# Attention then two 3x3 convolutions: the large attention pools on the other side of memory, and the last block's end put between the first bands

## The chip, the cores and the metric

The kernel runs on one core of a Trainium2 chip. The metric is device time in microseconds (us) of one execution, the median of several runs. The engines are named as in the profile: PE (TensorE, matmuls), PEld (its weight loads), DVE (VectorE), ACT (ScalarE), POOL (GpSimd) and SP (SyncE, which here only issues transfers).

## The reference

The input x has 4 images of 128 channels and 64 x 64 pixels, in float32. Two layers follow one another.

```python
# layer 0: attention with 4 heads of 32 channels over 4096 positions, scale = 32 ** -0.5
x_norm = group_norm(x, 8 groups)
q, k, v = split(qkv_w @ x_norm + qkv_b)
attn = softmax(q @ k.T * scale)
x = x + proj_w @ (attn @ v) + proj_b
# layer 1: a residual block of two 3x3 convolutions with weights quantized to 3 bits
residual = x
out = relu(batchnorm(conv3x3(x, quant(w1, alpha1))))     # statistics over batch and pixels
out = batchnorm(conv3x3(out, quant(w2, alpha2)))
return relu(out + residual)
```

## The kernel before

**Attention** runs over 32 blocks: 4 images, and in each 8 blocks of 512 queries. A block has 32 steps of 128 keys. In a step PE computes the scores of four heads (L442), ACT takes their exponential into a tile p of 128 x 4 x 512 (L444), and PE multiplies p with the values into `acc` (L456). The denominators of the softmax are sums of the p tiles over the steps. DVE adds most of them into a tile r (L469, L471); the p tiles of six steps (`MOVED`) are added by transfers that POOL issues, into a tile rm (L464, L466). The program's order is written out by hand: three halves of scores, then three halves of weights, and side work hung on half steps by `schedule` with `at_half` and `add`. The end of each block is side work of the next: `merge` adds rm to r by a transfer, `sums` multiplies r with ones on PE in two halves, ACT copies the result to `ls`, `spread` brings 4 rows of 512 into 128 x 16 by a transfer (lq), `invert` takes reciprocals (rq) and writes them to DRAM (rd), `gather` reads them back on all partitions (rc), `weigh` multiplies acc's copy with rc, `project` is the output projection on PE, and `store` adds bias and input on DVE and writes to `y0` in DRAM through POOL. The last block has no next one. For it `sums_at_once` runs totals of rm and r on PE and reciprocals of 128 x 512 on DVE, and `bounds` takes two maxima for the check value `worst`.

**Convolution layer 1** works on 16 bands (4 images, 4 bands of 16 rows). A band's input is split into a high and a low part. A plain band (`conv`, L828) takes 36 matmuls of 512 columns: two half bands, 9 taps, two parts. A mixed band (`conv_by_two`, L874) computes two rows at once from sums and differences of rows and takes 24. `mixed_parts` makes its inputs: vo and vi on DVE (L595 to L598), their high parts uo and ui on ACT (L600), the low parts lo and li on DVE (L604). `rows_of_two` puts the result together: a copy on ACT (L884), inner rows (L887, L888) and outer rows (L891, L893) on DVE; the squares for the batch norm follow on ACT (L957). A plain band takes its statistics on DVE (L969) and is copied by ACT (L970). The set `BY_TWO` says which bands are mixed; in the first layer before, band 2 is plain. The loop in `layer` prepares band m + 2 in the pass of band m (`parts_of`) and loads band m + 3 (`load_band`, on SP with border memsets on POOL).

**The seam** stands at L837 to L855. Bands 0 and 1 are convolved between the parts of the last block's end, band 2 is split, and then `att.close()` gives all attention pools back at once. The pools `mid` (results cv0 to cv3, the second layer's weights, the mixed weights `wmix`, the statistics) and `upper` (parts of mixed bands) take their memory. `mix_weights(0)` and six small operations on alpha (L904 to L906) follow, and then the loop. The pass of band 5 contains `count_bad`, with one small matmul `nbad` on PE (L1004).

**Memory.** Pools are allocated as a stack. A pool can be put on the left or on the right side (`side="right"`), each a stack of its own. By default an instruction that uses a new pool waits until everything in the released pools that it overlays is done; `reuse_waits="tile"` makes it wait only for the tiles that it overlays. The tiles of `kpool` (keys in attention, bands afterwards) stay in place throughout.

Of the kernel before, what the change touches and what calls it, by code (L numbers as in the profile page):

```python
# [78 lines left out]
def _fast_body(ctx, tc, x, norm_w, norm_b, qkv_wt, qkv_b, proj_wt, proj_b,  # L79
# [131 lines left out]
    y0 = [dram.tile([P, N], F32, name=f"y0_{b}") for b in range(B)]  # L211
    BR = 2 * RB
    KW = (BR + 2) * PW
    att = ExitStack()
    vpool = att.enter_context(tc.tile_pool(name="vpool", bufs=NB + 1))
    qpool = att.enter_context(tc.tile_pool(name="qpool", bufs=2))
    stage = att.enter_context(tc.tile_pool(name="stage", bufs=1))
    xpool = att.enter_context(tc.tile_pool(name="xpool", bufs=3))
    ppool = att.enter_context(tc.tile_pool(name="ppool", bufs=9))
# [253 lines left out]
    def finish_parts(n):  # L473

        b, qb = blocks[n]
        av = rpool.tile([P, FB], F32, name=f"av{n}", tag="av")
        rc = rpool.tile([P, FB], F32, name=f"rc{n}", tag="rc")
        t = {}

        def copy():  # L480
            nc.scalar.copy(av, acc[n])


        def total(r, first, end, cs=slice(0, FB)):
            if "l" not in t:
                t["l"] = psa.tile([P, FB], F32, name=f"l{n}", tag="a")
            for h in range(HEADS):
                nc.tensor.matmul(t["l"][h * D : (h + 1) * D, cs], ones, r[:, h, cs],  # L488
                                 start=first, stop=end)

        def merge():
            nc.gpsimd.dma_start(out=rsum[n], in_=msum[n], accum_op=ALU.add)  # L492

        def evacuate():
            t["ls"] = stage.tile([P, FB], F32, name=f"ls{n}", tag="ls")
            nc.scalar.copy(t["ls"], t["l"])
# [7 lines left out]
        def sums_at_once():  # L504
            total(msum[n], True, False)
            total(rsum[n], False, True)
            evacuate()
            for j in range(4):
                cs = slice(j * P, (j + 1) * P)
                nc.vector.reciprocal(rc[:, cs], t["ls"][:, cs])  # L510
            weigh()

        def bounds():
            most = [small.tile([P, 1], F32, name=f"most{i}") for i in range(2)]
            for u, m in zip((t["ls"], rc), most):
                nc.vector.tensor_reduce(m, u, AX.X, ALU.max)
                nc.vector.tensor_tensor(worst[:, 0:1], worst[:, 0:1], m, ALU.add)
# [14 lines left out]

        def gather():
            nc.sync.dma_start(out=rc, in_=t["rd"].unsqueeze(1).to_broadcast([HEADS, D, FB]))

        def weigh():
            nc.vector.tensor_tensor(av, av, rc, ALU.mult)

        def residual():
            t["x"] = load_x(b, qb)  # L540

        def project():
            t["o"] = psa.tile([P, FB], F32, name=f"po{n}", tag="a")
            banded(t["o"], wp, av)

        def store():
            nc.vector.scalar_tensor_tensor(t["x"], t["o"], bp, t["x"], ALU.add, ALU.add)
            nc.gpsimd.dma_start(out=y0[b][:, qb * FB : (qb + 1) * FB], in_=t["x"])

        return dict(copy=copy, merge=merge, sums=sums, sums_at_once=sums_at_once, bounds=bounds,  # L550
                    spread=spread, invert=invert, gather=gather,
                    weigh=weigh, residual=residual, project=project, store=store)

# [26 lines left out]

    BY_TWO = (set((3, 4, 6, 7, 9, 10, 12, 13, 14)), set((2, 3, 4, 6, 7, 9, 10, 12, 13, 14)))

    def mixed_parts(t, name):

# [94 lines left out]
    def schedule(n, before):  # L681
# [49 lines left out]
        if b + 1 < B:  # L731
# [8 lines left out]
                    at_half(ends[13 + 2 * i], late[b][1 + 2 * i])  # L740
                    at_half(ends[13 + 2 * i] + 3, late[b][2 + 2 * i])
            if qn == 2:
                at_half(ends[1], late[b][5])
                at_half(ends[1] + 1, late[b][6])
                at_half(ends[1] + 1, late[b][7])
                at_half(ends[1] + 2, late[b][8])
            if b == 0:
                chunks = {2: (), 3: (0, 1), 4: (2, 3), 5: (4, 5), 6: (6,), 7: (7,)}
            else:
# [108 lines left out]
    def mix_weights(i):  # L858

# [35 lines left out]

        return copy, inner, outer

    mix_weights(0)


    a_q, a_g, a_n = ([small.tile([P, 1], F32, name=f"{n}{i}") for i in range(2)]
                     for n in ("aq", "ag_", "an"))
    for i in range(2):
# [16 lines left out]
        nc.vector.tensor_tensor(a, r, a_g[i], ALU.mult)  # L920
        return a, c

    def layer(i, prepare, done):


        plain = [m for m in range(len(bandlist) - 1) if m not in BY_TWO[i]]
# [6 lines left out]
        n_plain, n_two = (float(len(u) * 2 * FB) for u in (plain, two))  # L933
        nc.gpsimd.memset(end[:, 0:1], n_plain)
        nc.gpsimd.memset(end[:, 3:4], n_two)
        for m, (b, g) in enumerate(bandlist[:-1]):
            begin, rest, later = prepare(m)
            if m in BY_TWO[i]:
                a = conv_tile(i, b, g)
                a = [a[:, j, :] for j in range(2)]  # L940
                if (len(two) - 1 - two.index(m)) % 2:
                    c = [psa.tile([P, FB], F32, name=f"c{i}_{b}_{g}{j}", tag="a") for j in "xy"]
                else:
                    c = pss.tile([P, 2, FB], F32, name=f"c{i}_{b}_{g}z", tag="s")
                    c = [c[:, j, :] for j in range(2)]
                conv_by_two(ready[i, b, g], a, c, i)
# [13 lines left out]
            ps = done[m] if m < len(done) else conv_tile(i, b, g)  # L960
            for j in range(2):
                if m >= len(done):
                    conv(ready[i, b, g], ps[:, j, :], j, wq[i])
            begin()
            rest()
            later()
            for j in range(2):
                c = 2 * g + j
                nc.vector.bn_stats(st[:, 2 * plain.index(m) + j, :], ps[:, j, :])  # L969
                nc.scalar.copy(cv[b][:, c * FB : (c + 1) * FB], ps[:, j, :])  # L970
            if m == 0:
                mv = small.tile([P, 2], F32, name=f"first{i}", tag="mv")
                nc.vector.bn_aggr(mv, st[:, 0:2, :].rearrange("p j s -> p (j s)"))
                nc.vector.tensor_copy(shift[:, 0:1], mv[:, 0:1])
                nc.vector.tensor_scalar(shift[:, 1:2], mv[:, 0:1], -1.0, None, ALU.mult)
# [21 lines left out]
    def count_bad():  # L997
# [6 lines left out]
        nc.tensor.matmul(nbad[0:1, 0:1], bad, ones[:, 0:1], start=True, stop=True)  # L1004
        nc.vector.tensor_copy(cnt, nbad[0:1, 0:1])

    def nothing():
        pass

    def first(m):  # L1010
        begin = rest = nothing
        if 0 < m and m + 2 < len(bandlist):
            begin, rest = parts_of(0, m + 2, raw[bandlist[m + 2]])

        def later():
            if m == 5:
                count_bad()
                raw["w"] = f32(stack_tile("raw_w"))[:, : TAPS * P].rearrange("p (t o) -> p t o", o=P)
                nc.sync.dma_start(out=raw["w"], in_=wqd)
            if m == 6:  # L1020
                nc.vector.tensor_copy(wq[1], raw["w"])
            if 0 < m < len(bandlist) - 3:
                load_band(*bandlist[m + 3])

        return begin, rest, later

    a1, c1 = layer(0, first, early)

    def relu_band(m):
        b, g = bandlist[m]  # L1030
# [29 lines left out]

    def load_res(b, i):
        if b < B - 2:
            t = mid.tile([P, HN], F32, name=f"res{b}_{i}")
# [18 lines left out]

        return begin, rest, later

    a2, c2 = layer(1, second, [])
    for b in (B - 2, B - 1):
        for i in range(4):
            load_res(b, i)
# [469 lines left out]
```

## Time and profile before

| | |
|---|---|
| median of 3 runs | 2505.38 us (2503.05 to 2505.57) |
| profiled execution | 2506.32 us, of which the span in the trace is 2504.6 us |
| PE, DVE, ACT busy | 98%, 88%, 86% of the span |
| attention ends (first conv matmul) | 2234.4 us |
| first convolution layer's last matmul ends | 2359.9 us |
| mean granted PE clock | 0.994 |

The span runs from the first to the last instruction in the trace. Times in the trace are counted from its start. The profiled execution lies 0.9 us above the median of the runs, so differences are taken against its own time and then carried to the median.

### The profile page before, as it was taken

The page shows a single profiled execution, that of the slowest core. Times are in us where ns is not written, and L with a number is a line of the kernel's source. Part 1 is how long each engine was busy: PE and PEld are TensorE (multiplying, and loading weights), DVE is VectorE, ACT ScalarE, POOL GpSimd, SP SyncE. Part 2 cuts the span into 40 slices and gives each one's busy share as a digit, 9 for nine tenths or more (in the row PEclk, how much of TensorE's full clock was granted, in tenths as well). Part 3 has the DMA queues.
Part 4 walks back from the last instruction along what each step waited for, and adds up shares of the span by engine and source line. Part 5 has one row for each costly group of instructions (what it writes and reads, how often), then busy time and mean ns, then how long its engine had stood idle before and what let it go on. Part 6 is the DMA issues. An engine that isn't in the chain of part 4 may idle for free. (4 is left out here: it accounts for less than half of the span.)

```text
span 2504.6 us, 64822 instructions
## 1 busy us (share of the span) xinstructions
PE 2459.0 (98%) x28480; PEld 1462.1 (58%) x28480; DVE 2206.2 (88%) x1552; ACT 2147.0 (86%) x2344; POOL 281.9 (11%) x463
## 2 busy tenths in 40 slices
PE   9999999999999999999999999999999999998995
PEld 6555555555555555555555555555555555566774
DVE  6899888898988888889988898889999999988797
ACT  5999888999988899999988898998999999964475
POOL 2111111111011111110011111110000000100000
PEclk9999999999999999999999999999999999999998
DMA  6777677787767666788767767688656656664205
GB/s 197 189 185 170 163 178 174 171 200 184 181 156 168 178 165 165 160 201 191 167 149 184 167 157 170 170 204 185 147 129 153 142 131 148 154 128 97 86 1 203
DMA packets 148954, 403.84 MB, mean 161 GB/s; under 512 B 59416, under 2 KB 60184, under 8 KB 120120
## 3 DMA queue, kind: packets, MB, share of 16 engines
q0 software_dynamic: 45840, 280.39, 49.0%
q1 hardware_dynamic: 100952, 113.60, 17.2%
q8 instruction: 225, 3.69, 0.6%
q10 hardware_dynamic: 1872, 5.64, 0.6%
q14 instruction: 65, 0.53, 0.1%
HBM read 107.48 MB, written 56.42 MB: 65 GB/s over the span
## 5 line engine op out<-in xcount | busy, mean ns | idle before, releaser
L444 ACT ACTIVATE p<-s 128x1024 f32<-128x1024 f32 x2048 | 1950.5, 1032 | 202.2 <-PE s L442 154.0
L471 DVE TENSOR_TENSOR r<-r,p 128x2048 f32<-128x2048 f32 x768 | 1758.2, 2289 | 65.3 <-ACT p L444 15.0
L442 PE MATMUL s<-q,k 64*128 64x512 f32 x8192 | 1139.7, 409 | 1.9 <-ACT p L444 1.7
L456 PE MATMUL acc<-p,v 128*32 128x256 f32 x16384 | 1026.6, 383 | 0.0
L442 PEld LDWEIGHTS s<-q,k 64*128 64x128 f32 x8192 | 715.7, 185 | 410.9 <-issue 166.1
L456 PEld LDWEIGHTS acc<-p,v 128*32 128x32 f32 x16384 | 462.8, 109 | 483.4 <-issue 248.4
L466 POOL DMA_DIRECT2D rm<-p x160 | 139.1, 869 | 799.4 <-ACT p L444 556.8
L352 DVE SCALAR_TENSOR_TENSOR kst<-pk,b,kst 128x512 fp32r<-128x512 f32 x32 | 24.0, 750 | 83.3 <-PE s L442 68.5
L469 DVE TENSOR_TENSOR r<-p,p 128x2048 f32<-128x2048 f32 x32 | 73.2, 2288 | 12.8 <-ACT p L444 12.8
L352 DVE SCALAR_TENSOR_TENSOR qst<-pq,b,qst 128x512 fp32r<-128x512 f32 x32 | 24.0, 751 | 58.5 <-PE s L442 47.5
L957 ACT ACTIVATE uo<-cv,shift 128x1024 fp32r<-128x1024 f32 x19 | 21.9, 1153 | 53.1 <-DVE cv L893 50.5
L356 POOL DMA_DIRECT2D qd<-qst x31 | 23.6, 761 | 266.7 <-DVE qst L352 225.3
L828 PE MATMUL c<-hi,wq 128*128 128x512 f32 x198 | 51.2, 403 | 1.2 <-ACT hi L1045 1.2
L828 PE MATMUL c<-lo,wq 128*128 128x512 f32 x198 | 50.8, 401 | 0.0
L492 POOL DMA_DIRECT2D r<-rm x31 | 26.2, 844 | 218.2 <-PE s L442 61.8
L970 ACT COPY cv<-c 128x512 f32<-128x512 f32 x22 | 12.9, 586 | 38.4 <-DVE st L969 38.4
L828 PEld LDWEIGHTS c<-hi,wq 128*128 128x128 f32 x198 | 36.9, 188 | 13.1 <-issue 2.1
L828 PEld LDWEIGHTS c<-lo,wq 128*128 128x128 f32 x198 | 37.3, 188 | 10.0
L874 PE MATMUL c<-ui,wmix 128*128 128x512 f32 x114 | 35.2, 418 | 6.8 <-ACT cv L970 4.2
L356 POOL DMA_DIRECT2D kd<-kst x27 | 20.0, 740 | 178.6 <-DVE kst L352 169.9
L351 ACT ACTIVATE kst<-pk,b 128x512 fp32r<-128x512 f32 x32 | 22.3, 699 | 18.1 <-PE pk L317 18.0
L488 PE MATMUL l<-r,ones 128*32 128x256 f32 (+1 forms) x504 | 37.7, 383 | 0.0
(258 smaller groups left out, 1137.1 us busy)
## 6 DMA issues: line engine op xcount, KB each, us to landing
rm<-p POOLq DMA_DIRECT2D x192, 1024.0 KB, 7.8
q<-qd SPq DMA_DIRECT2D x248, 128.0 KB
r<-rm POOLq DMA_DIRECT2D x31, 1024.0 KB, 7.6
x<-in_x_dram SPq DMA_DIRECT2D x86, 256.0 KB
k<-kd SPq DMA_DIRECT2D x124, 128.0 KB
qd<-qst POOLq DMA_DIRECT2D x31, 512.0 KB, 5.6
kd<-kst POOLq DMA_DIRECT2D x27, 512.0 KB, 4.7
y<-x POOLq DMA_DIRECT2D x32, 256.0 KB, 6.1
```

Of the source, the lines that this page charges most:

```text
L352: nc.vector.scalar_tensor_tensor(lo, ps[what], bias, t[:, 0, :], ALU.add, ALU.subtract)
L356: (nc.sync if start else nc.gpsimd).dma_start(out=dst[b, j].rearrange("s p n -> p s n"), in_=t)
L442: nc.tensor.matmul(s[:, i, :], k[r, half, c0 : c0 + P], q[r, half, part, :], start=(part == 0), stop=(part == 1))
L444: nc.scalar.activation(pts[step][:, 2 * half : 2 * half + 2, :], s, AF.Exp, scale=SCALE)
L456: nc.tensor.matmul(acc[n][h * D : (h + 1) * D, cs], v[:, kt % KB, h * D : (h + 1) * D], pt[:, h, cs], start=(kt == 0 and half == 0), stop= ...
L466: nc.gpsimd.dma_start(out=msum[n], in_=pt, accum_op=ALU.add)
L469: nc.vector.tensor_tensor(rsum[n], pts[step - 1], pt, ALU.add)
L471: nc.vector.tensor_tensor(rsum[n], rsum[n], pt, ALU.add)
L488: nc.tensor.matmul(t["l"][h * D : (h + 1) * D, cs], ones, r[:, h, cs], start=first, stop=end)
L492: nc.gpsimd.dma_start(out=rsum[n], in_=msum[n], accum_op=ALU.add)
L828: nc.tensor.matmul(ps.rearrange("p (r w) -> p r w", w=W), w[:, tap, :], part[:, r0 + kh : r0 + kh + RB, kw : kw + W], start=(n == 0), stop ...
L874: nc.tensor.matmul(ps.rearrange("p (r w) -> p r w", w=W), w[:, kw, :], part[m][:, :, kw : kw + W], start=(n == 0), stop=(n == 5))
```

## The change

1. vpool, qpool and ppool (values, queries, p tiles) go to the right side, in a stack of their own (`core`), which is released first. `mid`, now with two results cv0 and cv1, and `upper` are allocated there with waits by tile. The results cv2 and cv3 and the residual tiles go to a pool `low` on the left, allocated after the rest of attention has been given back, in the pass of band 3.
2. The last block's end uses the same steps as the other blocks (merge, sums, spread, invert, gather, weigh), in a function `opening` that places them between the work on bands 0, 1 and 2. Project and store come in the pass of band 3.
3. Band 2 of the first layer is mixed.
4. Four small side tasks of the group norm (`late[b][5]` to `late[b][8]`) move by a few half steps.

```diff
-    att = ExitStack()
-    vpool = att.enter_context(tc.tile_pool(name="vpool", bufs=NB + 1))
-    qpool = att.enter_context(tc.tile_pool(name="qpool", bufs=2))
+    core, att = ExitStack(), ExitStack()
+    vpool = core.enter_context(tc.tile_pool(name="vpool", bufs=NB + 1, side="right"))
+    qpool = core.enter_context(tc.tile_pool(name="qpool", bufs=2, side="right"))
+    ppool = core.enter_context(tc.tile_pool(name="ppool", bufs=9, side="right"))
...
-    BY_TWO = (set((3, 4, 6, 7, 9, 10, 12, 13, 14)), set((2, 3, 4, 6, 7, 9, 10, 12, 13, 14)))
+    BY_TWO = (set((2, 3, 4, 6, 7, 9, 10, 12, 13, 14)), set((2, 3, 4, 6, 7, 9, 10, 12, 13, 14)))
...
-                at_half(ends[1], late[b][5])
-                at_half(ends[1] + 1, late[b][6])
-                at_half(ends[1] + 1, late[b][7])
-                at_half(ends[1] + 2, late[b][8])
+                at_half(ends[0], late[b][5])
+                at_half(ends[0] + 1, late[b][6])
+                at_half(ends[2], late[b][7])
+                at_half(ends[2] + 1, late[b][8])
...
-    early = [conv_tile(0, *bandlist[m]) for m in range(2)]
-    last = parts[len(blocks) - 1]
-    conv(ready[0, 0, 0], early[0][:, 0, :], 0, wq[0])
-    last["residual"]()
-    conv(ready[0, 0, 0], early[0][:, 1, :], 1, wq[0])
-    split_band(*bandlist[2])
-    load_band(*bandlist[3])
-    last["sums_at_once"]()
-    conv(ready[0, 0, 1], early[1][:, 0, :], 0, wq[0])
-    conv(ready[0, 0, 1], early[1][:, 1, :], 1, wq[0])
-    last["project"]()
-    last["store"]()
-    last["bounds"]()
-    att.close()
-    mid = ctx.enter_context(tc.tile_pool(name="mid", bufs=1))
-    cv = [mid.tile([P, N], F32, name=f"cv{b}") for b in range(B)]
+    core.close()
+    mid = ctx.enter_context(tc.tile_pool(name="mid", bufs=1, side="right", reuse_waits="tile"))
+    cv = [mid.tile([P, N], F32, name=f"cv{b}") for b in range(2)]
     wq.append(mid.tile([P, TAPS, P], F32R, name="wq1"))
-    upper = ctx.enter_context(tc.tile_pool(name="upper", bufs=12))
     wmix = mid.tile([P, 2, 3, P], F32R, name="wmix")
+    upper = ctx.enter_context(tc.tile_pool(name="upper", bufs=12, side="right", reuse_waits="tile"))
...
-    mix_weights(0)
...
+        def stats(m, j, ps):
+            nc.vector.bn_stats(st[:, 2 * plain.index(m) + j, :], ps[:, j, :])
+        def keep(m, j, ps):
+            nc.scalar.copy(cv[b][:, c * FB : (c + 1) * FB], ps[:, j, :])
...
         def later():
+            if m == 3:
+                last = parts[len(blocks) - 1]
+                last["project"]()
+                last["store"]()
+                att.close()
+                pools["low"] = ctx.enter_context(tc.tile_pool(name="low", bufs=1, reuse_waits="tile"))
+                cv.extend(pools["low"].tile([P, N], F32, name=f"cv{b}") for b in (2, 3))
...
+    def opening(banks, stats, keep, origin):
+        last = parts[len(blocks) - 1]
+        last["merge"]()
+        e = [conv_tile(0, *bandlist[m]) for m in range(2)]
+        conv(ready[0, 0, 0], e[0][:, 0, :], 0, wq[0])
+        begin, rest = parts_of(0, 2, raw[bandlist[2]])
+        begin()
+        load_band(*bandlist[3])
+        stats(0, 0, e[0])
+        keep(0, 0, e[0])
+        conv(ready[0, 0, 0], e[0][:, 1, :], 1, wq[0])
+        mix_weights(0)
+        rest()
+        last["residual"]()
+        stats(0, 1, e[0])
+        keep(0, 1, e[0])
+        origin()
+        conv(ready[0, 0, 1], e[1][:, 0, :], 0, wq[0])
+        last["sums"](0)
+        last["sums"](1)
+        last["spread"]()
+        begin, rest = parts_of(0, 3, raw[bandlist[3]])
+        begin()
+        load_band(*bandlist[4])
+        conv(ready[0, 0, 1], e[1][:, 1, :], 1, wq[0])
+        stats(1, 0, e[1])
+        keep(1, 0, e[1])
+        last["invert"]()
+        last["gather"]()
+        rest()
+        stats(1, 1, e[1])
+        keep(1, 1, e[1])
+        done = banks(2)
+        conv_by_two(ready[0, 0, 2], *done, 0)
+        begin, rest = parts_of(0, 4, raw[bandlist[4]])
+        begin()
+        last["weigh"]()
+        rest()
+        load_band(*bandlist[5])
+        return {0: None, 1: None, 2: done}
```

More of the change, by code (lines that the diff above doesn't have):

```diff
@@ L213, in _fast_body @@
     KW = (BR + 2) * PW
-    att = ExitStack()
-    vpool = att.enter_context(tc.tile_pool(name="vpool", bufs=NB + 1))
-    qpool = att.enter_context(tc.tile_pool(name="qpool", bufs=2))
+    core, att = ExitStack(), ExitStack()
+    vpool = core.enter_context(tc.tile_pool(name="vpool", bufs=NB + 1, side="right"))
+    qpool = core.enter_context(tc.tile_pool(name="qpool", bufs=2, side="right"))
+    ppool = core.enter_context(tc.tile_pool(name="ppool", bufs=9, side="right"))
     stage = att.enter_context(tc.tile_pool(name="stage", bufs=1))
     xpool = att.enter_context(tc.tile_pool(name="xpool", bufs=3))
-    ppool = att.enter_context(tc.tile_pool(name="ppool", bufs=9))
     rpool = att.enter_context(tc.tile_pool(name="rpool", bufs=1))
@@ L501, in sums @@
                 evacuate()
[L504 to L517, printed above, removed]
         def spread():
@@ L548, in store @@
             nc.gpsimd.dma_start(out=y0[b][:, qb * FB : (qb + 1) * FB], in_=t["x"])
-        return dict(copy=copy, merge=merge, sums=sums, sums_at_once=sums_at_once, bounds=bounds,
+        return dict(copy=copy, merge=merge, sums=sums,
                     spread=spread, invert=invert, gather=gather,
@@ L921, in batch_norm, with layer @@
         return a, c
-    def layer(i, prepare, done):
+    def layer(i, prepare, start=None):
         plain = [m for m in range(len(bandlist) - 1) if m not in BY_TWO[i]]
@@ L935, in layer, with origin, banks @@
         nc.gpsimd.memset(end[:, 3:4], n_two)
+        def stats(m, j, ps):
+            nc.vector.bn_stats(st[:, 2 * plain.index(m) + j, :], ps[:, j, :])
+        def keep(m, j, ps):
+            b, g = bandlist[m]
+            c = 2 * g + j
+            nc.scalar.copy(cv[b][:, c * FB : (c + 1) * FB], ps[:, j, :])
+        def origin():
+            mv = small.tile([P, 2], F32, name=f"first{i}", tag="mv")
+            nc.vector.bn_aggr(mv, st[:, 0:2, :].rearrange("p j s -> p (j s)"))
+            nc.vector.tensor_copy(shift[:, 0:1], mv[:, 0:1])
+            nc.vector.tensor_scalar(shift[:, 1:2], mv[:, 0:1], -1.0, None, ALU.mult)
+        def banks(m):
+            b, g = bandlist[m]
+            a = conv_tile(i, b, g)
+            if (len(two) - 1 - two.index(m)) % 2:
+                c = [psa.tile([P, FB], F32, name=f"c{i}_{b}_{g}{j}", tag="a") for j in "xy"]
+            else:
+                c = pss.tile([P, 2, FB], F32, name=f"c{i}_{b}_{g}z", tag="s")
+                c = [c[:, j, :] for j in range(2)]
+            return [a[:, j, :] for j in range(2)], c
+        done = start(banks, stats, keep, origin) if start else {}
         for m, (b, g) in enumerate(bandlist[:-1]):
+            if m in done and m not in BY_TWO[i]:
+                continue
             begin, rest, later = prepare(m)
             if m in BY_TWO[i]:
[L939 to L942, printed above, removed]
-                else:
-                    c = pss.tile([P, 2, FB], F32, name=f"c{i}_{b}_{g}z", tag="s")
-                    c = [c[:, j, :] for j in range(2)]
-                conv_by_two(ready[i, b, g], a, c, i)
+                if m in done:
+                    a, c = done[m]
+                else:
+                    a, c = banks(m)
+                    conv_by_two(ready[i, b, g], a, c, i)
                 y = cv[b][:, 2 * g * FB : (2 * g + 2) * FB]
@@ L959, in layer @@
                 continue
-            ps = done[m] if m < len(done) else conv_tile(i, b, g)
+            ps = conv_tile(i, b, g)
             for j in range(2):
-                if m >= len(done):
-                    conv(ready[i, b, g], ps[:, j, :], j, wq[i])
+                conv(ready[i, b, g], ps[:, j, :], j, wq[i])
             begin()
@@ L967, in layer @@
             for j in range(2):
-                c = 2 * g + j
-                nc.vector.bn_stats(st[:, 2 * plain.index(m) + j, :], ps[:, j, :])
-                nc.scalar.copy(cv[b][:, c * FB : (c + 1) * FB], ps[:, j, :])
+                stats(m, j, ps)
+                keep(m, j, ps)
             if m == 0:
[L972 to L975, printed above, removed]
+                origin()
         nc.vector.bn_aggr(end[:, 1:3], st.rearrange("p j s -> p (j s)"))
@@ L1005, in count_bad @@
         nc.vector.tensor_copy(cnt, nbad[0:1, 0:1])
+    pools = {}
     def nothing():
@@ L1011, in first @@
         begin = rest = nothing
-        if 0 < m and m + 2 < len(bandlist):
+        if 2 < m < len(bandlist) - 2:
             begin, rest = parts_of(0, m + 2, raw[bandlist[m + 2]])
         def later():
+            if m == 3:
[5 more added lines that the diff above has]
+                cv.extend(pools["low"].tile([P, N], F32, name=f"cv{b}") for b in (2, 3))
             if m == 5:
@@ L1021, in later @@
                 nc.vector.tensor_copy(wq[1], raw["w"])
-            if 0 < m < len(bandlist) - 3:
+            if 2 < m < len(bandlist) - 3:
                 load_band(*bandlist[m + 3])
         return begin, rest, later
-    a1, c1 = layer(0, first, early)
+    def opening(banks, stats, keep, origin):
[14 more added lines that the diff above has]
+        keep(0, 1, e[0])
+        origin()
+        conv(ready[0, 0, 1], e[1][:, 0, :], 0, wq[0])
[21 more added lines that the diff above has]
+        return {0: None, 1: None, 2: done}
+    a1, c1 = layer(0, first, opening)
     def relu_band(m):
@@ L1062, in load_res @@
         if b < B - 2:
-            t = mid.tile([P, HN], F32, name=f"res{b}_{i}")
+            t = pools["low"].tile([P, HN], F32, name=f"res{b}_{i}")
         elif b == B - 2:
@@ L1083, in second @@
         return begin, rest, later
-    a2, c2 = layer(1, second, [])
+    a2, c2 = layer(1, second)
     for b in (B - 2, B - 1):
```

## The prediction

> **What bounds the kernel now.** I read the page first, then the table of windows over the seam between attention and the first convolution layer, then the timelines of TensorE (PE) and VectorE (DVE) in that seam. The page:
>
> ```profile
> span 2504.6 us, 64822 instructions
> PE 2459.0 (98%) x28480; PEld 1462.1 (58%) x28480; DVE 2206.2 (88%) x1552; ACT 2147.0 (86%) x2344; POOL 281.9 (11%) x463
> ```
>
> PE is busy 98% of the span, so a change that leaves the number of matmuls alone can win only where PE waits or runs slowly. The windows (length, busy time of PE, PEld, DVE, ACT, POOL, granted clock, DMA share, GB/s) show where that is:
>
> ```profile
> 2254.80:2263.70 8.90, 8.86 (x40) 6.68 (x36) 7.42 (x21) 1.17 (x2) 1.06 (x8) 1.00 0.39 96
> 2263.70:2266.30 2.60, 0.03 (x1) 0.03 (x1) 2.60 (x5) 2.14 (x2) 0.17 (x2) 1.00 0.01 2
> 2266.30:2273.30 7.00, 6.53 (x24) 4.26 (x24) 6.35 (x9) 3.32 (x4) 0.24 (x3) 1.00 0.42 90
> 2273.30:2276.90 3.60, 0.00 (x1) 0.01 (x1) 2.27 (x3) 1.23 (x3) 0.00 (x0) 0.81 0.70 147
> 2276.90:2284.90 8.00, 8.00 (x23) 6.27 (x24) 7.46 (x12) 5.00 (x7) 0.24 (x3) 0.66 0.26 75
> 2293.80:2359.90 66.10, 66.10 (x279) 51.99 (x279) 52.42 (x87) 29.75 (x41) 1.07 (x13) 1.00 0.47 125
> ```
>
> The reader is to see two holes in PE's work (2.6 and 3.6 us), a granted clock of 0.66 just after the second, and from 2293.8 to the layer's end no hole at all. PE's timeline names what the holes wait for, and the band after them takes 1.5 us for three matmuls instead of 0.9:
>
> ```profile
> 2266.27 0.98 PE L874 MATMUL c<-ui,wmix 128*128 128x512 f32 x3 [2.62 <-ACT ui L600]
> 2276.90 1.65 PE L874 MATMUL c<-ui,wmix 128*128 128x512 f32 x3 [3.61 <-ACT cv L970]
> 2293.81 0.19 PE L1004 MATMUL nbad<-ones,bad 128*1 128x1 f32 x2
> ```
>
> ACT is late because DVE is. DVE's timeline of the same stretch, whose waits are in brackets:
>
> ```profile
> 2231.03 7.08 DVE L471 TENSOR_TENSOR r<-r,p 128x2048 f32<-128x2048 f32 x3
> ...
> 2245.77 3.39 DVE L510 RECIPROCAL rc<-ls 128x128 f32<-128x128 f32 x4 [5.54 <-ACT ls L496]
> 2249.19 0.69 DVE L537 TENSOR_TENSOR av<-av,rc 128x512 f32<-128x512 f32 x1
> 2254.95 0.75 DVE L547 SCALAR_TENSOR_TENSOR x<-po,bp,x 128x512 f32<-128x512 f32 x1 [5.07 <-PE po L317]
> ...
> 2258.54 1.03 DVE L865 SCALAR_TENSOR_TENSOR wmix<-wq,wsum 128x384 fp32r<-128x384 f32 x2 [0.40 <-DMA y<-x]
> ...
> 2260.14 0.69 DVE L969 BATCH_NORM_STATS2 st<-c 128x6 f32<-128x512 f32 x1
> 2277.36 0.69 DVE L887 TENSOR_TENSOR cv<-cv,c 128x512 f32<-128x512 f32 x1 [1.14 <-ACT cv L884]
> ```
>
> DVE waits 5.5 us for the last block's sums and 5.1 us for its projection, and the first statistics of band 0, whose matmuls ended at 2243.2, come at 2260.1: they stand behind the projection, the store and everything that lies where attention lay.
>
> **The skill.** The Trainium skill, "TensorE: Matmul & The Clock Gate", Part 1, What's actually happening, says that a free-running window of about 3.4 us with PE idle halves its clock and a busy one restores it. The trace agrees on the length: the clock is 0.5 from 2275.5 to 2282.3, twice 3.41 us. It adds a threshold: the window that ended at 2275.5 was idle for 2.2 us and dropped; the one ending at 2265.3 was idle for 1.6 us and did not. "PSUM — Partial Sum Buffer", Engine vs sequencer instructions: the queues of ScalarE, VectorE and GpSimd are strict FIFO. That is what the 5-us waits show, and I order each engine's work as the program has it. "DMA: Bandwidth & Descriptors", Issuing engines are not separate DMA queues: all transfers share 16 engines and interleave. The trace agrees: the 8 KB lq<-ls takes 1.5 us to its last packet alone, up to 7.1 us with an rm<-p in flight.
>
> **The change, part by part.** First PE. From its first conv matmul, at 2234.37, I add what it must do up to the small nbad matmul, after which the two kernels issue the same work:
> - band 0, two convs: 8.79 (2234.37 to 2243.16); one conv of band 1: 4.40.
> - the sums: eight halves of a total in place of the sixteen-matmul pair of totals (1.85), so 0.93.
> - the other conv of band 1: 4.40. Band 2 becomes mixed, 24 matmuls in 5.77 (2299.78 to 2305.55) in place of 36 in 8.84. Band 3: 5.77. The projection, moved here: 1.00. Band 4: 5.77. Band 5: 8.64.
>
> The sum is 45.47, so PE could reach nbad at 2279.8, against 2293.8: **14.0 us at most**: 6.5 of holes, 2.4 of slow clock (12 matmuls in 5.28 instead of 2.88), 3.1 of band 2, 0.9 of sums, the rest small waits.
>
> Second DVE, which starts after the last sum at 2238.11 (2231.03 + 7.08). Durations are gaps between starts in the timeline, since neighbours overlap by about 0.08:
> - six little operations on alpha, now in front: 0.65. Mixing band 2 (vo, vi, vi): 2.41. Statistics 0.66. Mixed weights 1.89. The low parts of band 2: 2.36. Statistics 0.66, origin 0.38. Mixing band 3: 2.41. Statistics 0.66. That is 12.08, so DVE comes to the inversion at 2250.2.
> - there it waits for the spread sums. PE has them at 2234.37 + 8.79 + 4.40 + 0.93 = 2248.5, ACT's copy is out 0.73 later (as 2245.01 to 2245.74), lq takes 1.53 and some 0.15 of semaphore: 2250.9. **A wait of 0.7.** Behind it on DVE stand the low parts of band 3 and all of band 4.
> - inversion 0.40, low parts 2.36, statistics 0.66, mixing band 4 2.41, weigh 0.65, low parts 2.36: 2259.7. Inner rows of band 2: 1.33; outer rows 1.21: 2262.3.
> - band 3's inner rows need ACT's copy L884, which stands on ACT behind band 2's squares: 0.18 + 1.15 + 0.57 + 0.05, so they start at 2264.25 instead of 2277.36.
> - from there to nbad DVE ran without a hole (2277.36 to 2293.8, 16.4 us), with the same operations as afterwards, plus the store now in front of band 3's outer rows: 0.70.
>
> So nbad comes 2277.36 - 2264.25 - 0.70 = **12.4 us earlier**, at 2281.4. DVE, not PE, sets it; PE waits 1.6 us there, less than the 2.2 that dropped the clock and as much as the 1.6 that did not. After nbad PE was full, so the shift stays to the end.
>
> Third, what is hidden, and under what. The reciprocal of 128x512 (3.39) and the two maxima go; 128x16 pieces and three small transfers replace them. The merge (a POOL transfer, median 7.6) starts when r is complete, at 2238.2, and lands at 2245.8; PE asks for it at 2247.6, so 1.8 us of cover, and what it is late beyond that moves PE, lq and DVE alike. On SP, lq waits for ls, and band 4's load, rd and rc stand behind it: load 4 is out at 2249.8 and down 3.9 later, at 2253.7; rd 1.0 later; rc 1.3 after that, 2255.4 with issue; DVE wants band 4 at 2254.3 and rc at 2256.7. Band 3's load was already issued at 2222.4 and stays early; SP runs ahead. On POOL the border memsets of band 3 follow the merge's issue (2239.1; wanted at 2244), those of band 6 the store's issue (2269; wanted at about 2269): no more than 0.5 if late. The new pools on the right overlay v, q and p, whose last reader is the DVE add that ends at 2238.1; the lower pool's first use is band 8. I cost the placement at nothing.
>
> Fourth, inside attention: the small norm matmuls at L281 and L291 move a few half steps. One of three places had PE waiting 0.9 us (DVE b, at 736.8). That goes; but in that block the first matmul now comes in the same group as the copy of acc, which ended at 731.24 when PE was free at 730.2: 1.1 new. Net +0.2; bounds -0.9 and +1.5.
>
> The sum: 2504.6 - 12.4 + 0.2 = 2492.4 of span; with the 1.7 around it (2506.32 - 2504.6) 2494.1. The profiled execution is 0.9 over the median of the runs, so the forecast against 2505.38 is **2493.2 us**.
>
> **The rivals.**
> - *DVE arrives later, and the clock drops.* If the sums or lq land 1.5 us late (lq's own range goes that far), PE waits 3.1 at nbad, more than the threshold, and band 6 runs at half clock for one window, 1.7 to 2.4 us. For it: a transfer chain that once was spread over 25 us is squeezed into 7. Against it: POOL has nothing else in flight then. Gain 12.2 - 1.5 - 2.1 = 8.6: about 2497.
> - *PE becomes the bound*, if the tail of DVE is shorter than I add up: 14.0, so 2491.4.
> - *Slower: the accumulating transfers from p at its new place.* Each of 31 blocks has six moves and a merge on one chain: 4.8 + 5 x 8.4 + 7.6 = 54.4 us of a block of 69.1, so 14.7 of slack, 2.1 per transfer. If a transfer from the other side of memory took more than 2.1 us longer (over 25%), each block would grow by seven times the excess; at 2.16 that eats the 12.2 us gained, at 2.2 it is about 2514. For it: ACT already waits for these transfers in five places, 4.0 us. Against it: nothing in the profile ties a transfer's time to its address, and the rows of 8 KB stay.
> - *The tile-by-tile waits do nothing.* Then all of mid waits for the end of v, q and p, 2238.1, where DVE starts anyway: no change to the forecast.
>
> **How the numbers follow.** A measurement of this kernel can tell 0.2%, 5 us, from no change. Forecast 0.64 (2491.5 to 2495 alone); late DVE with slow clock 0.20; PE bound 0.06; slower 0.07; and 0.03 for a transfer penalty near its threshold that eats most of the gain. Faster 0.90, same 0.03, slower 0.07. The range reaches from PE's bound less 1 us of scatter to the second case with 2 us more: 2490.5 to 2499.
>
> **What would show it.** Right: nbad about 12 us earlier; no hole over 2 us on PE before it, one of 1 to 2 just before it; clock 1.00 through the seam; band 2 with 24 matmuls; DVE waiting under 2 us at the reciprocal of rq; the block length of attention unchanged at 69. Wrong: PE waiting at the sums (merge late), a clock under 1 after nbad, DVE waiting for rc or band 4's load, longer rm<-p.

## The result, and the profile after

| | before | after |
|---|---|---|
| median of 12 runs each | 2505.40 us (2503.05 to 2507.79) | 2504.73 us (2500.67 to 2508.73) |
| profiled execution, and its span | 2506.32, 2504.6 | 2501.34, 2499.6 |
| first conv matmul starts | 2234.37 | 2230.46 |
| from there to nbad | 59.44 | 59.15 |
| from there to the end of layer 1 | 125.75 | 125.24 |

The ratio is 0.9996, with an interval of 0.9987 to 1.0005. The change did not move the time by anything that can be measured; the forecast was 2493.2. Below, "the layer" is the stretch from the first conv matmul to the small matmuls that follow the layer's last one. The profiled execution of after is 3.4 us below its own median: attention ended 3.9 us earlier in it, in small steps scattered over the blocks, and the layer gained only 0.5. The start of the layer lies anywhere between 2230.5 and 2234.4 in the traces of this study, so I compare lengths counted from it.

The page after:

```profile
span 2499.6 us, 64813 instructions
...
PE 2452.0 (98%) x28468; PEld 1463.4 (59%) x28468; DVE 2205.0 (88%) x1554; ACT 2150.3 (86%) x2347; POOL 282.3 (11%) x464
...
L811 PE MATMUL c<-hi,wq 128*128 128x512 f32 x180 | 48.4, 415 | 5.3 <-ACT cv L909 4.0
```

PE has 12 matmuls fewer and is busy 7 us less, so band 2 is mixed as said. The last line is new: the plain convolution now waits 4.0 us for ACT's copy at L909. The windows of after over the seam (length, busy time of PE, PEld, DVE, ACT, POOL, granted clock, DMA share, GB/s):

```profile
2230.50:2235.00 4.50, 4.50 (x20) 3.27 (x18) 4.33 (x9) 0.59 (x1) 0.44 (x1) 1.00 0.34 97
2235.00:2239.00 4.00, 0.01 (x1) 0.00 (x0) 3.93 (x7) 2.63 (x3) 0.66 (x4) 0.77 0.81 164
2239.00:2245.60 6.60, 6.57 (x18) 5.16 (x19) 3.19 (x4) 0.00 (x0) 0.24 (x3) 0.62 0.30 60
2267.00:2270.20 3.20, 0.00 (x0) 0.00 (x0) 3.17 (x7) 0.00 (x0) 0.00 (x0) 1.00 1.29 228
2270.20:2278.60 8.40, 8.38 (x33) 5.96 (x34) 6.53 (x12) 4.08 (x7) 0.93 (x6) 0.80 0.37 94
2287.30:2289.60 2.30, 0.04 (x1) 0.00 (x0) 2.22 (x4) 0.70 (x1) 0.17 (x2) 1.00 0.00 0
```

The holes of before are gone, and three others stand in their place: 4.0, 3.2 and 2.3 us. After the first two the clock is low. PE's timeline names what each waited for:

```profile
2239.03 4.21 PE L811 MATMUL c<-hi,wq 128*128 128x512 f32 x9 [4.02 <-ACT cv L909]
...
2270.22 1.06 PE L317 MATMUL po<-av,wp 128*32 128x512 f32 x8 [3.23 <-DVE cv L860]
...
2289.61 0.19 PE L990 MATMUL nbad<-ones,bad 128*1 128x1 f32 x2 [2.27 <-DVE bad L988]
```

The first is the odd one. These nine matmuls are the second half of band 0. They use input that has long been there and write a bank that nobody reads. The copy which they wait for is of the other half:

```profile
2238.40 0.58 ACT L909 COPY cv<-c 128x512 f32<-128x512 f32 x1
```

DVE's timeline shows the same thing the other way round, with statistics that wait for matmuls:

```profile
2227.18 7.08 DVE L471 TENSOR_TENSOR r<-r,p 128x2048 f32<-128x2048 f32 x3
...
2237.25 0.69 DVE L904 BATCH_NORM_STATS2 st<-c 128x6 f32<-128x512 f32 x1
...
2245.88 0.70 DVE L904 BATCH_NORM_STATS2 st<-c 128x6 f32<-128x512 f32 x1 [3.69 <-PE c L811]
...
2255.59 0.70 DVE L904 BATCH_NORM_STATS2 st<-c 128x6 f32<-128x512 f32 x1 [6.12 <-PE c L811]
2256.21 0.23 DVE L510 RECIPROCAL rq<-lq 128x16 f32<-128x16 f32 x1
...
2265.21 0.69 DVE L520 TENSOR_TENSOR av<-av,rc 128x512 f32<-128x512 f32 x1 [3.16 <-DMA rc<-rd]
```

At 2255.59 DVE takes the statistics of band 1's first half, whose matmuls ended at about 2250.0. It waits until 2255.56, when the second half ends. `invert` stands behind it in DVE's queue, so rq comes 25.75 us after the layer's start instead of the forecast 16.5 (2250.9 - 2234.37). `weigh` then waits 3.2 us for rc, and the projection on PE 3.2.

The lengths add up. PE's list of the prediction is 45.47 us. The holes are 4.02 + 3.23 + 2.27 = 9.5. The slow clock costs 2.2 (18 matmuls in 6.58 instead of 4.40) and 1.6 (band 4's 24 matmuls in 7.36 instead of 5.77). Together 58.8, against 59.15 measured.

### The profile page after: what moved, and what is told of

It is laid out like the page before. It is cut to its first block, busy times and chain, and to the rows that moved or that the text cites. A ratio compares the mean times of both kernels' runs of the same rounds, so it can differ in the third digit from the quotient of the medians.

```text
span 2499.6 us, 64813 instructions
## 1 busy us (share of the span) xinstructions
PE 2452.0 (98%) x28468; PEld 1463.4 (59%) x28468; DVE 2205.0 (88%) x1554; ACT 2150.3 (86%) x2347; POOL 282.3 (11%) x464
## 5 line engine op out<-in xcount | busy, mean ns | idle before, releaser
L466 POOL DMA_DIRECT2D rm<-p x160 | 139.1, 870 | 796.7 <-ACT p L444 618.3
L317 PE MATMUL po<-av,wp 128*32 128x512 f32 x256 | 33.4, 593 | 4.6 <-DVE cv L860 3.2
L488 PE MATMUL l<-r,ones 128*32 128x256 f32 x512 | 37.7, 379 | 0.0
L464 POOL DMA_DIRECT2D rm<-p x32 | 17.9, 558 | 174.1 <-DMA r<-rm 82.3
```

The source lines that it names most:

```text
L317: nc.tensor.matmul(out[cs, :], w[:, cs], x, start=True, stop=True)
L466: nc.gpsimd.dma_start(out=msum[n], in_=pt, accum_op=ALU.add)
```

## The experiments

**Theory.** The program orders a tile's uses by whole tile. Both halves of a band (`e[0][:, 0, :]`, `e[0][:, 1, :]`) are one tile. In band 0, after puts the statistics and the copy of the first half in front of the matmuls of the second, so PE waits for ACT. In band 1 the program has both halves' matmuls first; there DVE comes to the first half's statistics before the second half has run, and waits for PE. **Rivals:** that the order or the new memory does it in another way (an overlaid buffer, transfers that land late), or that DVE simply has more to do than I added up. All experiments start from after unless said otherwise. A ratio is to the median of the kernel before, measured beside the run.

**Band 0's order alone.**

```diff
-        stats(0, 0, e[0])
-        keep(0, 0, e[0])
         conv(ready[0, 0, 0], e[0][:, 1, :], 1, wq[0])
         mix_weights(0)
         rest()
         last["residual"]()
+        stats(0, 0, e[0])
+        keep(0, 0, e[0])
         stats(0, 1, e[0])
```

> The changed kernel with the statistics and the copy of band 0's first half put behind both of the band's convolutions. Theory 1 (a read of one half of a PSUM tile and a write of its other half wait for each other): PE's 4.0 us hole in band 0 and the 2.2 us of slow clock after it go, and from the first conv matmul to nbad it takes about 53 us instead of 59.2. Theory 2 (ACT's copy is late because of where it writes, or PE waits for the release of a buffer): the hole stays or moves to band 1, 58 to 59 us.

Measured: 51.93 us to nbad, the layer 118.03; median 2495.14, ratio 0.9965 (0.9951 to 0.9978). PE's timeline:

```profile
2238.58 2.30 PE L811 MATMUL c<-hi,wq 128*128 128x512 f32 x9
...
2266.72 1.06 PE L317 MATMUL po<-av,wp 128*32 128x512 f32 x8 [2.48 <-DVE cv L860]
```

The second half now follows the first without a wait. Two lines moved return 7.2 us of the layer: the hole of 4.0, the slow clock behind it, and the part of the second hole that came from it.

**Band 1's order alone.**

```diff
-        stats(1, 0, e[1])
-        keep(1, 0, e[1])
         last["invert"]()
         last["gather"]()
         rest()
+        stats(1, 0, e[1])
+        keep(1, 0, e[1])
         stats(1, 1, e[1])
```

> The changed kernel with the statistics and the copy of band 1's first half put behind the inversion and the low parts of band 3. Theory 1: DVE's 6.1 us wait for band 1's second convolution goes from in front of the inversion; what is left there is the wait for the spread sums, about 3.4 us; rd still queues behind band 4's load, so first conv to nbad shrinks by only 1 to 2 us, to about 58. Theory 2 (the transfer chain alone sets the inversion): no change, 59.

Measured: 58.05 to nbad, but the layer 125.77, no shorter than after's 125.24; median 2503.12, ratio 0.9991 (0.9985 to 0.9998). The waits of PE (engine, line, what it waited for, total, times, longest) keep the hole of band 0:

```profile
PE c L811 <- ACT cv L909: 4.0, 1, 4.0
PE nbad L990 <- DVE bad L988: 3.3, 1, 3.3
PE po L317 <- DVE cv L860: 1.8, 1, 1.8
```

DVE no longer waits for PE before `invert`, but then waits 4.2 us there for lq, since PE comes to the sums late. The hole at the projection shrinks from 3.2 to 1.8, and the one at nbad grows from 2.3 to 3.3, with a slow clock of 3.41 us behind it. Band 1's order is no bound of its own.

**Both orders.** The two edits together.

> Both moves. Theory 1: 6.2 us of band 0 and 1 to 2 us of band 1, so first conv to nbad in about 51 to 52 us, run about 7 us faster than the kernel before. What remains is the wait for rc, whose packets share the rings with the loads of bands 5 and 6, with the projection behind it. Theory 2: 57 to 59 us, no gain over before.

Measured: 50.60 to nbad, the layer 118.31; median 2496.48, ratio 0.9966 (0.9954 to 0.9977). DVE's timeline:

```profile
2251.06 0.25 DVE L510 RECIPROCAL rq<-lq 128x16 f32<-128x16 f32 x1 [0.76 <-DMA lq<-ls]
...
2260.50 0.69 DVE L520 TENSOR_TENSOR av<-av,rc 128x512 f32<-128x512 f32 x1 [2.23 <-DMA rc<-rd]
```

Its layer starts 0.06 from that of before, so the times can be laid beside the forecast directly: the reciprocal was forecast at 2250.9 with a wait of 0.7. The next step misses: rc was to be there at 2255.4, and its last packet lands at 2259.68.

PE's waits in the same run:

```profile
PE nbad L990 <- DVE bad L988: 3.3, 1, 3.3
PE po L317 <- DVE cv L860: 1.1, 1, 1.1
...
```

The clock is slow for 3.41 us from 2285.78, behind nbad. So what band 1's order gains before nbad is lost after it: the layer is no shorter than with band 0's order alone (118.03).

**After's order with two tiles.** This is the test against the rival of the order: nothing moves, the second half of band 0 gets a tile of its own.

```diff
+        other = pss.tile([P, 2, FB], F32, name="c0_0_0w", tag="s")
...
-        conv(ready[0, 0, 0], e[0][:, 1, :], 1, wq[0])
+        conv(ready[0, 0, 0], other[:, 1, :], 1, wq[0])
...
-        stats(0, 1, e[0])
-        keep(0, 1, e[0])
+        stats(0, 1, other)
+        keep(0, 1, other)
```

> The changed kernel in its own order, but band 0's two halves lie in two different PSUM tiles. Theory 1 (the dependence is by tile, not by bank or by order): PE's 4.0 us hole goes, first conv to nbad about 53 us, as with the reads moved. Theory 2 (PE waits for a buffer or for ACT's place in its queue): the hole stays, about 59 us.

Measured: 51.08 to nbad, the layer 118.48; median 2498.14, ratio 0.9975 (0.9964 to 0.9985). PE's timeline:

```profile
2236.10 2.32 PE L811 MATMUL c<-lo,wq 128*128 128x512 f32 x9
2238.26 2.30 PE L811 MATMUL c_0w<-hi,wq 128*128 128x512 f32 x9
```

The wait is gone although the statistics and the copy still stand in front. DVE reads c at 2240.63, in the middle of the matmuls on c_0w, and ACT copies c at 2241.78. So the wait was for the tile. The Trainium skill, "PSUM — Partial Sum Buffer", PSUM bank collisions raise a hardware error, says that accesses of two engines to different banks run clean, and that the guard should go by bank and quadrant. This run agrees: it reads one bank while PE writes another, with no wait. The 4.0 us came from a guard that goes by tile.

**What makes rc late.** After both orders, the path from rd to `weigh` is the next. First, on top of both orders, bands 4 and 5 loaded earlier, so that their transfers are out of rc's way:

```diff
         last["residual"]()
+        load_band(*bandlist[4])
+        load_band(*bandlist[5])
...
-        load_band(*bandlist[4])
...
-        load_band(*bandlist[5])
```

> The kernel with both reads moved, and the loads of bands 4 and 5 issued before the sums instead of beside the small transfers. If rc is late because its packets share the rings with those loads, rc lands about 1.5 us after its issue, DVE's 2.2 us wait in front of weigh goes, and first conv to nbad takes about 48.4 us instead of 50.6. If rc is late by its own length or because rd is, the wait stays, 50 to 51 us. The run follows nbad only as far as the slow clock after it does.

Measured: 49.65 to nbad, the layer 117.28; median 2495.93, ratio 0.9965 (0.9951 to 0.9978), 1.0 us of the layer better than both orders alone. The 1.5 us expected for rc were missed: its transfer (issue to last packet) took 6.2 us in after, 5.2 with both orders, and still 5.1 here. It has 128 packets of 2 KB. SP runs ahead, so that a band's load of half a megabyte in packets of 256 bytes goes out right behind rc whichever bands were loaded before: 1562 such packets moved between rc's issue and its last packet, against 1636 with both orders. So this run did not take the loads away from rc, and that they are what makes it long is not shown. The traces speak against them as the only cause. rc's first packet starts only 1.3 to 1.4 us after the issue in all of them, and in three attention blocks of before, where its packets can be told from all others and no band is loaded (issues at 1809.74, 1943.53 and 2008.88), it took 5.6 to 6.2 too, with a transfer in packets of 8 KB under way. What was gained here came from a shorter way from rd to rc's issue (1.4 instead of 3.1), and the earlier loads delayed lq in turn (last packet 2.1 after its issue, instead of 1.55):

```profile
2250.23 0.25 DVE L510 RECIPROCAL rq<-lq 128x16 f32<-128x16 f32 x1 [1.63 <-DMA t<-y]
...
2257.85 0.69 DVE L520 TENSOR_TENSOR av<-av,rc 128x512 f32<-128x512 f32 x1 [0.41 <-DMA rc<-rd]
```

Second, both orders with `weigh` behind the inner rows of band 2, so that other work covers rc:

```diff
-        last["weigh"]()
...
+            if m == 2:
+                parts[len(blocks) - 1]["weigh"]()
             if m == 3:
                 last = parts[len(blocks) - 1]
```

> The kernel with both reads moved, and weigh put behind the low parts of band 4 and the inner rows of band 2, so that the work behind it on DVE no longer waits for rc. Expected: rc lands as late as before (about 2260), DVE's wait for it under 0.5 us, first conv to nbad about 48.5 us. If rc sets the end through the projection instead, PE waits at the projection 2 us longer and nbad gains under 1 us.

Measured: 48.33 to nbad, the layer 116.03; median 2494.41, ratio 0.9959 (0.9944 to 0.9975). rc took 5.3 us, but nobody waits for it. The wait at the projection is gone, and one remains:

```profile
PE nbad L990 <- DVE bad L988: 2.8, 1, 2.8
```

**The hole at nbad.** The early loads, the late `weigh`, and `count_bad` moved from the pass of band 5 to that of band 8:

```diff
-            if m == 5:
+            if m == 8:
                 count_bad()
+            if m == 5:
```

> Both reads moved, the loads early, weigh late, and the check with nbad moved from the pass of band 5 to that of band 8. The nbad matmul stands later here, so the first layer is measured from its first conv matmul to its last: 125.5 us before. If PE's hole at nbad and the slow clock after it are only the price of that one matmul behind DVE, PE runs through and the layer takes about 112 to 114 us, 11 to 13 us less than before. If DVE is the bound beyond nbad too, the hole appears at a band's PSUM buffers instead, and the layer takes 115 us or more.

This expectation was missed: the layer took 117.75, 1.7 longer than the run before it, which does not have the early loads either; median 2495.75, ratio 0.9959 (0.9946 to 0.9973). PE's timeline:

```profile
2301.24 0.19 PE L990 MATMUL nbad<-ones,bad 128*1 128x1 f32 x2 [2.88 <-DVE bad L988]
2301.36 1.65 PE L843 MATMUL c<-ui,wmix 128*128 128x512 f32 x3
```

The hole only moved, and the clock fell behind it for 6.8 us (1.65 for three matmuls), where it was 3.4 in the run before. nbad needs what DVE does at the end of its list in that same pass, so PE drained down to DVE at both places of the pair. The remedy is distance between the two. With both orders and the late `weigh`, DVE's part stays in pass 5, and the matmul and its copy go to pass 8:

```diff
             if m == 5:
-                count_bad()
+                raw["bad"] = count_bad()
+            if m == 8:
+                count_rest(raw["bad"])
```

> Reads moved and weigh late, and of the check only the matmul nbad and what follows it moved to the pass of band 8; its two DVE operations stay in the pass of band 5, so that DVE has them done long before PE asks. Theory: the hole at nbad is a PE instruction placed directly behind the end of DVE's list for that pass; without it PE has enough prepared and runs through. First layer about 111.5 us (116.0 less the 2.8 us hole and 1.9 us of slow clock), run about 2490 us. Rival: DVE is the bound of the layer, the hole moves to a PSUM buffer or to the parts of a band, 114 us or more.

Measured: the layer 111.73; median 2490.30, ratio 0.9941 (0.9927 to 0.9954). One window of it, from the first conv matmul almost to the layer's end:

```profile
2234.00:2345.70 111.70, 111.70 (x484) 86.33 (x483) 96.09 (x157) 49.76 (x67) 4.13 (x35) 1.00 0.53 126
```

PE has no hole and no slow clock. This is the ceiling of the prediction: before's 125.75 less "14.0 us at most" is 111.75.

The same split in after, with nothing else:

> The changed kernel with only the nbad matmul moved to the pass of band 8, its DVE operations left. The 2.3 us hole at nbad goes; the holes in band 0 and at the projection and the slow clock after them stay. First layer about 123 us instead of 125.2. Rival (the hole only moves on): 125.

Measured: the layer 121.78; median 2499.82, ratio 0.9978 (0.9970 to 0.9987). The waits of PE in the layer are the one of the tile and, at the projection, the one that follows DVE's wait for rc:

```profile
PE c L811 <- ACT cv L909: 4.0, 1, 4.0
PE po L317 <- DVE cv L860: 2.7, 1, 2.7
PE c_0y L843 <- DVE x L530: 0.3, 1, 0.3
```

**Placement alone.** This one starts from before: v, q and p on the right with `mid` and `upper` over them by tile, cv2, cv3 and the residual tiles in `low`; the last block's end, band 2 and the norm's side tasks as before.

> The kernel before with the placement alone: values, queries and p tiles on the right, the new pools there and on the left with waits by tile, the last block's end as it was. The forecast's fourth rival, read for this part: placement costs and brings nothing, attention's block length stays, first conv to nbad 59 us (at most 0.4 us less, the wait of the mixed weights), same time as before. The third rival: rm<-p takes over 2 us longer and each block grows.

Measured: 59.08 to nbad and the layer 125.21 (before 59.44 and 125.75); median 2503.29, ratio 0.9993 (0.9984 to 1.0001). The placement costs nothing and brings at most half a microsecond. Attention ended no later (at 2231.08), and the median rm<-p took 7.8 us from issue to landing, as in before, so no penalty on its transfers shows.

**Band 2 alone.** The best version so far with band 2 plain again:

```diff
-    BY_TWO = (set((2, 3, 4, 6, 7, 9, 10, 12, 13, 14)), set((2, 3, 4, 6, 7, 9, 10, 12, 13, 14)))
+    BY_TWO = (set((3, 4, 6, 7, 9, 10, 12, 13, 14)), set((2, 3, 4, 6, 7, 9, 10, 12, 13, 14)))
...
```

> The kernel with reads moved, weigh late and nbad's matmul moved, but band 2 plain as before the change. PE gets 12 matmuls more (3.1 us), DVE about 4.7 us less (mixing and rows of two 7.4, against a low part and two statistics). If PE sets the layer by then, 114.5 us, 3 us longer than with the mixed band. If DVE does, the same or shorter, 111 us.

Measured: the layer 114.46 against 111.73; median 2492.26, ratio 0.9948 (0.9933 to 0.9964). PE waits nowhere in the layer of this run either. So band 2 mixed is worth 2.7 us once PE is the bound, near the 3.1 forecast.

**The tile in every plain band.** In the loop and in `opening` of the version with the split (band 2 mixed), both statistics ahead of both copies, so that the second statistics don't wait for the first copy:

```diff
-                stats(m, j, ps)
-                keep(m, j, ps)
+                stats(m, j, ps)
+            for j in range(2):
+                keep(m, j, ps)
```

> As the kernel with nbad's matmul moved, and in plain bands both statistics come ahead of both copies, so that DVE does not wait for ACT's copy between them (0.65 us each time). DVE comes to the inversion and to band 3's rows about 1.3 us earlier. If PE sets the first layer, nothing changes there (within 0.5 us), and the second layer, whose start is in the chain that ended last with these pairs in it, may gain up to 1 us. If DVE sets the first layer, it gains 1.3 us.

Measured: the layer 111.73 as before this edit; median 2489.95, ratio 0.9937 (0.9924 to 0.9951). DVE's waits for the copy at L909, 4.0 us in the layer with the split, are gone. PE was already full in the layer, so this buys nothing there. The rest of the program after the layer took 143.2 against 143.9 or more elsewhere; over the runs the step is within the scatter. The last versions are faster than both kernels.

## Why the prediction was wrong, point by point

- **PE's list, 45.47 us and "14.0 us at most": right.** The layer without holes takes 111.73; the list was complete and its durations held. What failed is that the conditions for running it gapless weren't examined: waits between the two halves of one tile stood in the forecast at nothing, without a reason.
- **"Band 0, two convs: 8.79": the step that failed first.** It took the time of two convs back to back for two convs with a read of the same tile written between them. They took 15.15 us in after (2230.46 to 2245.61), from the hole of 4.0 and the slow clock of 2.2. Shown by moving the read, and by the second tile. Forecast for the layer was 12.4 less than before, 113.3; after took 125.2. With both orders it took 118.3, so 6.9 of the 11.9 us missing go with the tile; the other 5.0 are PE's waits at the projection and at nbad, as far as they go beyond the 1.6 forecast, and the slow clock behind nbad.
- **"DVE comes to the inversion at 2250.2, there it waits 0.7": failed by the same omission.** I priced statistics at 0.66 each and gave them no wait. The wait was 6.1 us with `invert` behind it. With both orders the reciprocal came at 2251.06 with a wait of 0.76, so the rest of that sum was right. This wait was not what set the time, though: taken away alone it left the layer at 125.8.
- **The signal stood in the trace of before, and I did not read it as one.** Groups by line:

```profile
L969 DVE BATCH_NORM_STATS2 st<-c 128x6 f32<-128x512 f32 x22 | 15.3, 695 | 7.8 <-ACT cv L970 7.3 <-PE c L828 0.6
...
L970 ACT COPY cv<-c 128x512 f32<-128x512 f32 x22 | 12.9, 586 | 38.4 <-DVE st L969 38.4
```

Statistics that only read wait 7.3 us for copies that only read, the second half's for the first half's. Nothing in the data asks for that. It fits a guard by tile, and it is gone in the last run, where no copy stands between the two statistics. Before had both halves' matmuls ahead of both reads, so PE never met it.

- **"rc 1.3 after that": mis-sized.** It took 6.2 us (5.1 to 5.3 in three other runs). The traces have 1.3 to 1.4 us from rc's issue to its first packet, not to its last. A band's load goes out behind it and their packets interleave, which the prediction cited and didn't apply to rc; how much of the length that explains stays open. DVE waited 3.2 us for rc in after, and PE as long at the projection; the wait lies off the path when `weigh` comes later. Read in a row, the terms of that sum (2253.7, 1.0, 1.3) also give 2256.0, not 2255.4; that is still before DVE's 2256.7.
- **"DVE sets nbad, PE waits 1.6": right in kind, short in size.** The wait was 2.3 in after and 2.3 to 3.3 in the runs with the order mended and `count_bad` whole. With the split it is gone.
- **Held:** band 2 (2.7 of 3.1); the merge is hidden, PE doesn't wait at the sums, with both orders neither; placement at nothing; the new wait of 1.1 us at L281 inside attention, which the trace has at 1.11 (`gb` waits for ACT's av at 728.84).
- **The rivals.** "DVE arrives later, and the clock drops" has the right direction and the wrong cause: I let the transfer of the sums be late, but DVE was held by its own statistics, and the clock fell at band 0 and at the projection, not at nbad. With both orders, though, its picture appears: PE waits 3.3 at nbad where the rival had 3.1, a slow stretch of one window follows, and the median is 2496.5 where it had about 2497; what comes late there is rc, not the sums. The rival of longer transfers falls with the placement run. No case of mine left the time unchanged through a wait that the new order itself creates.

## What to carry to other kernels

When reads and writes of parts of one buffer are put in a new order, ask first what the unit of the program's own guard is: reads of two different parts that wait for each other in a profile suggest that it is the whole tile. Either keep all writes of a tile ahead of its reads, and the reads late enough that the last write is done when their engine comes to them, or give the parts tiles of their own. And when one engine fills the holes of another, look for the instruction that joins their queues, like nbad here: the later engine's whole backlog appears there, and here moving the pair didn't help, while separating its producer from its consumer did.

## What the runs showed of the hardware

**The clock.** The length of a hole alone doesn't say whether the clock falls: holes of 2.5 us (band 0's order alone) and of 2.3 (placement, with one of 0.3 in the same window) were followed by a slow clock, holes of 2.6 (before) and 2.7 (after with the split) were not. Where a trace has several falls, they lie whole multiples of 3.41 us apart (in after, 2237.15 and 2271.28). Counting windows of 3.41 back from each trace's last fall gives the idle time of PE in every window. In all fourteen traces, each window in which PE idled for 1.97 us or more was followed by a slow one. Of those with less, which reach up to 1.92, one was (1.68, placement). Here are two windows of before, the second of them just ahead of its slow clock, and last one of the run of band 0's order, ahead of the slow clock there (length, then PE's busy time):

```profile
2261.86:2265.27 3.41, 1.80 (x8) 1.09 (x6) 3.34 (x8) 1.78 (x3) 0.04 (x2) 1.00 0.53 111
2272.10:2275.51 3.41, 1.18 (x5) 0.58 (x4) 2.77 (x3) 1.46 (x2) 0.11 (x3) 1.00 0.74 158
...
2264.75:2268.16 3.41, 1.44 (x10) 0.55 (x11) 2.49 (x6) 0.79 (x1) 0.00 (x0) 1.00 1.10 182
```

Up to the end of the layer, a slow stretch lasted one window where PE idled in its first window for at most 0.34 us, and two (6.83) where it idled for 0.69 to 1.88. Those of before and after in the layer cost 1.6 to 2.4 each. No run moved a hole against the windows by itself, and the trace models where matmuls end, so this stays a reading of the traces.

**A transfer of 256 KB.** rc, in rows of 2 KB, took 4.9 to 6.2 us from issue to last packet at its place in the layer, with a band's load in packets of 256 bytes behind it on the same queue, and 5.6 to 6.2 in three attention blocks with a transfer in packets of 8 KB instead. The first 1.3 to 1.4 of that pass before its first packet. Nothing here shows it alone.
